# A two-layer graph transformer on one core: the second table laid out by rank, stored by ScalarE's queue, and the edges' node numbers turned into ranks on TensorE

## The chip, the cores and the metric

The kernel runs on one core of a Trainium2 chip. The metric is the device time of one execution in microseconds (us), the median of three runs. One execution was also recorded by the hardware profiler, and every statement about where time goes rests on that record. The engines are called as in the profile: PE is TensorE (PEld its weight loads), DVE is VectorE, ACT is ScalarE, POOL is GpSimd, and SP is SyncE, which here only issues DMAs.

## The reference, cut to what matters

There are 6250 nodes of 128 features and 100,000 edges. A node has one of 16 types, an edge one of 32. Two layers run one after the other; in each, with 8 heads of 16 features:

```
k, q, v = x @ Wk[type], x @ Wq[type], x @ Wv[type]          # per node
kT = einsum('nhd,htdo->nhto', k, Watt)                      # per node and edge type
vT = einsum('nhd,htdo->nhto', v, Wmsg)
a  = (kT[src, :, etype] * q[dst]).sum(-1) * pri[:, etype].T / 4
att = softmax of a over the edges that end in the same node
hag = segment_sum(vT[src, :, etype] * att, dst)
h  = silu(hag @ Wa[type])
h  = h * sigmoid(skip[type]) + x * (1 - sigmoid(skip[type]))
x  = layernorm(h) * g + b
```

The output is `layernorm(x0 + (x2 @ ff_w + ff_b))`, where x0 is the input and x2 the result of the second layer.

## The kernel before

**Tables.** For each layer l the kernel writes a table `tabs[l]` in HBM. A node has 32 rows in it, one for each edge type, and a row holds the 128 numbers of kT and the 128 of vT (1 KB). One table has 6272 x 32 rows, 205 MB. An edge is served by gathering row `32 * node(src) + etype`. These row numbers are made once, in `kvi`, and are put into the tile `ell` (128 partitions, one column per slot) during the preparation.

**Ranks, blocks and superblocks.** The nodes are sorted into ranks 0 to 6271 by class of type and number of incoming edges (`rank_order`, lines 641 to 863). A block is 128 consecutive ranks, one per partition; there are 49 blocks, and block b has `KB[b]` slots, which is how many incoming edges its nodes may have (block 44, called `TOP`, has 28 slots of gathers and a way of its own for the rest). Over all blocks there are 819 slots. One slot is one indirect DMA of POOL that fetches 128 rows, one per partition (line 1324). Blocks are grouped into 15 superblocks of two to four (`sbs`, lines 1073 to 1087), with 83, 63, 37, 48, 83, 63, 37, 39, 83, 63, 37, 37, 63, 37 and 46 slots, in this order of work.

**Preparation (0 to 652 us).** It sorts the nodes, builds the first table (PE products in `table_block`, copies from PSUM to the tile `st`, scatters by POOL at line 1024), and fills `ell`, `neg` and the like (`limits_of`, lines 865 to 947, runs in steps beside the gathers of `ell`).

**Edges (`edges`, line 1127), once per layer.** For each block the slots are gathered in groups of four into one of twelve buffers `kv` (line 1320). After each gather POOL sets two small tiles `pause` to zero (line 1330). VectorE multiplies a group by the query (line 1344) and sums per head (line 1350). When a block's scores are complete, `finished` (line 1189) runs in steps beside the next block: maximum, exponential on ScalarE (line 1213), weighted sums of the vT half (lines 1229 to 1257). So a group's buffer is held until the next block is under way. In layer 1 the query, the exponentials and the products sit in a PSUM tile of two banks, a pair, from the pool `tps`, which has three such pairs (`query`, line 1171).

**Nodes (`nodes`, line 1426).** When a superblock's last block is done, its node work is put on the list `work` and goes on in steps beside the next superblock: normalization, typed product with Wa, tanh, layer norm. In layer 0 it also makes the next k, v and q and hands k and v to `pieces_of` (line 1568), which makes the second table's rows for that superblock; in layer 1 it ends with the last product and the result.

**The second table's way to HBM.** `pieces_of` walks through `table_block` (line 262): for each block twice (16 edge types at a time) PE makes the products in pairs of `tps`, ScalarE copies them to `st` (line 281; 2 MB, three buffers), and the tile is put on a list `late`. Eight steps later `scatter` (line 1555) lets POOL write it with an indirect DMA to the rows of the nodes, whose numbers are in `row2`. All 98 scatters must have landed before the first gather of layer 1.

**What sets the order.** POOL's instructions run in the order written in the code. On the other engines a scheduler orders them at compile time, following the order of the code; at run time each engine works strictly in order and waits on semaphores. `tick` (line 1140) decides in which slot a step of `work` or `pieces` is written: each entry has a pace in steps per slot, and only the first entry of a list moves.

The steps of the prediction touch lines 1324 and 1330 (gather and pause), 1344 and 1350 (products and sums per slot group), 1213 (exponential), 274 and 281 (table products and copies), 1556 (scatter), 1177 (query into a pair), 237 and 251 (typed products), 1519 and 1123 (rows h and q out and back in by SP), 1525 and 1527 (last bias and residual).

## Time and profile before

| | us |
|---|---|
| median of three runs | 3402.58 (3395.8 to 3412.61) |
| profiled execution | 3402.78 |
| its span, first to last instruction | 3400.7 |
| preparation | 0 to 652 |
| gathers of layer 0 | 652 to 2050 |
| tail of layer 0 | 2050 to 2120 |
| gathers of layer 1 | 2120 to 3351 |
| tail of layer 1 | 3351 to 3401 |

The stages are read from the first and last gather of each layer. A row of a group in the profile gives line, engine, operation, output and inputs, shape and count, then after a bar the busy time in us and the mean of one in ns, then after a second bar the engine's idle time just before these instructions and what ended most of it. "issue" as a releaser means that the record shows nothing that the engine waited for, and "remote" a semaphore whose source it does not show. A row of the waits gives who waited for whom, the total in us, how often, and the longest.

### The profile page before, as it was taken

How to read it: one execution, taken by the hardware profiler on the slowest of the kernel's cores; microseconds unless marked ns; L12 is line 12 of the kernel's file. 1: busy time of each engine (PE TensorE's matmuls, PEld its weight loads, DVE VectorE, ACT ScalarE, POOL GpSimd, SP SyncE). 2: the span in 40 equal slices, each digit the busy share in tenths (PEclk: the TensorE clock that was granted, in tenths of full speed). 3: DMA queues.
4: the chain of work that ended last, by engine and by line, in shares of the span. 5: the costliest groups of instructions: out<-in, count | busy, mean ns of one | idle time of the engine just before them, and what ended most of it. 6: DMA issues, size and time to landing. Idle time of an engine off the chain costs nothing. (4 is left out here: it accounts for less than half of the span.)

```text
span 3400.7 us, 24784 instructions
## 1 busy us (share of the span) xinstructions
PE 1668.8 (49%) x5291; PEld 745.2 (22%) x5291; DVE 1864.6 (55%) x4307; ACT 1035.4 (30%) x1720; POOL 2394.8 (70%) x5400
## 2 busy tenths in 40 slices
PE   5899999403676657776667565011211122012112
PEld 2444444201232322232222222000110011001001
DVE  8626642156655666566655543356555565566555
ACT  2778754200444123423334434001100120012111
POOL 2232367588878877788777772888788888888874
PEclk8888976556676768777777667555555555555555
DMA  6899989833677456766667768333333333333331
GB/s 178 364 417 412 406 324 347 272 89 95 236 260 269 140 183 250 270 243 211 215 246 277 269 241 320 99 94 99 99 95 97 98 107 100 90 101 100 92 88 45
DMA packets 169096, 674.80 MB, mean 198 GB/s; under 512 B 52972, under 2 KB 83726, under 8 KB 143886
## 3 DMA queue, kind: packets, MB, share of 16 engines
q0 software_dynamic: 114144, 638.40, 52.7%
q1 hardware_dynamic: 38402, 27.55, 2.9%
q10 hardware_dynamic: 16384, 7.11, 0.9%
q14 instruction: 120, 0.98, 0.1%
q8 instruction: 46, 0.75, 0.1%
HBM read 248.64 MB, written 425.02 MB: 198 GB/s over the span
## 5 line engine op out<-in xcount | busy, mean ns | idle before, releaser
L1324 POOL DMA_INDIRECT kv<-tab,ell x1638 | 1639.9, 1001 | 339.3 <-issue 286.0
L281 ACT COPY st<-tb 128x512 f32<-128x512 f32 (+1 forms) x1108 | 745.1, 761 | 548.2 <-PE tb L274 275.2
L1344 DVE TENSOR_TENSOR kv<-kv,tb 128x512 f32<-128x512 f32 (+3 forms) x223 | 142.9, 641 | 466.6 <-DMA kv<-tab,ell 446.5
L1330 POOL MEMSET pause<- 128x32 bf16 x3276 | 335.0, 141 | 67.9 <-remote 49.7
L259 PE MATMUL nb<-ident,hag 128*128 128x128 f32 x98 | 25.5, 396 | 714.7 <-DVE hag L1391 576.5
L1024 POOL DMA_INDIRECT tab<-st,rows x98 | 100.1, 1021 | 280.0 <-ACT st L281 251.2
L274 PE MATMUL tb<-bdv,kvT 32*128 32x512 f32 x784 | 254.0, 815 | 86.4 <-ACT st L281 53.7
L1350 DVE TENSOR_REDUCE a<-kv 128x32 f32<-128x512 f32 (+2 forms) x446 | 281.7, 634 | 6.9 <-DVE den L1219 1.2
L274 PE MATMUL tb<-bdv,vT 32*128 32x512 f32 x784 | 270.1, 782 | 8.6 <-ACT st L281 6.5
L251 PE MATMUL nb<-xm,wa 128*128 128x512 f32 (+2 forms) x336 | 191.7, 730 | 159.0 <-DVE xm L237 113.7
L274 PE MATMUL tb<-bdk,kvT 32*128 32x512 f32 x784 | 246.8, 809 | 42.7 <-ACT st L281 24.0
L1344 DVE TENSOR_TENSOR kv<-kv,q 128x512 f32<-128x512 f32 (+3 forms) x223 | 142.6, 642 | 215.5 <-DMA kv<-tab,ell 199.2
L274 PE MATMUL tb<-bdk,kT 32*128 32x512 f32 x784 | 242.6, 806 | 6.7 <-ACT st L281 3.0
L237 DVE SCALAR_TENSOR_TENSOR xm<-ntb,nb 128x512 f32<-128x512 bf16 (+2 forms) x304 | 156.4, 562 | 141.9 <-remote 85.8
L1556 POOL DMA_INDIRECT tab<-st,row x98 | 107.8, 1100 | 172.0 <-ACT st L281 139.4
L259 PEld LDWEIGHTS nb<-ident,hag 128*128 128x128 f32 x98 | 15.2, 196 | 733.9 <-issue 538.5
L1503 PE MATMUL nb<-xm,wkqv 128*128 128x512 f32 (+2 forms) x312 | 150.2, 646 | 45.0 <-DVE xm L237 30.9
L1177 ACT COPY tb<-hq 128x128 f32<-128x128 f32 x49 | 13.1, 269 | 460.0 <-DVE sums L1257 325.0
L251 PEld LDWEIGHTS nb<-xm,wa 128*128 128x128 f32 x336 | 88.4, 281 | 262.3 <-DVE xm L237 133.8
L251 PE MATMUL nb<-xm,wq 128*128 128x384 f32 (+2 forms) x168 | 84.5, 653 | 119.0 <-DVE a L1201 91.4
L259 PE MATMUL nb<-ident,hs 128*128 128x128 f32 x98 | 35.3, 464 | 218.0 <-DVE hs L1464 157.0
L274 PEld LDWEIGHTS tb<-bdv,vT 32*128 32x128 f32 x784 | 109.7, 221 | 107.6 <-ACT st L281 68.8
(336 smaller groups left out, 2740.3 us busy)
## 6 DMA issues: line engine op xcount, KB each, us to landing
kv<-tab,ell POOLq DMA_INDIRECT x1638
hr<-xrd SPq DMA_DIRECT2D x14, 256.0 KB
hqd<-hs SPq DMA_DIRECT2D x7, 512.0 KB
hq<-hqd SPq DMA_DIRECT2D x7, 512.0 KB
xrd<-xr POOLq DMA_DIRECT2D x10, 256.0 KB
hr<-xrd SPq DMA_DIRECT2D x10, 192.0 KB
hqd<-hs SPq DMA_DIRECT2D x5, 384.0 KB
hq<-hqd SPq DMA_DIRECT2D x5, 384.0 KB
```

The lines of the kernel that those rows point to most:

```text
L237: nc.vector.scalar_tensor_tensor(xm[:, :n], ntb[:, :n], float(t), hT[:, :n], op0=ALU.is_equal, op1=ALU.mult)
L251: nc.tensor.matmul(ps[:, :n], w[:, t, :], xm[:, :n], start=(t == types[0]), stop=(t == types[-1]))
L259: nc.tensor.transpose(tr[:, i * P:(i + 1) * P], src_of(i), ident)
L274: nc.tensor.matmul(pt[:, b], yT[s, i * P:(i + 1) * P], bd[s, tt, :], start=True, stop=True)
L281: nc.scalar.copy(to, pt)
L1024: put = nc.gpsimd.indirect_dma_start(out=tabs[0].rearrange("(n t) c -> n (t c)", t=16), out_offset=bass.IndirectOffsetOnAxis(ap=rows1[:, t ...
L1324: get = nc.gpsimd.indirect_dma_start(out=kv[:, j - j0, :], out_offset=None, in_=tabs[l][:], in_offset=bass.IndirectOffsetOnAxis(ap=ell[:, ...
L1330: nc.gpsimd.memset(pause[:, at % PAUSES, half], 0.0)
L1344: nc.vector.tensor_tensor(kk, kk, of.unsqueeze(1).to_broadcast([P, c, D]), op=ALU.mult)
L1350: nc.vector.tensor_reduce(to, kk.rearrange("p k (h d) -> p k h d", h=H), axis=AX.X, op=ALU.add)
L1503: nc.tensor.matmul(ps[:, :n], wkqv[:, j, t, :], xm[:, :n], start=(t == types[0]), stop=(t == types[-1]))
L1556: put = nc.gpsimd.indirect_dma_start(out=tabs[1].rearrange("(n t) c -> n (t c)", t=16), out_offset=bass.IndirectOffsetOnAxis(ap=row2[:, tg ...
```

## The change

The second table is laid out by rank and no longer by node. A superblock's ranks are consecutive, so a stored tile of 128 nodes goes to 128 places with a fixed distance of 32 KB, and a plain DMA on ScalarE's queue, issued right after the tile's last copy, takes the place of POOL's indirect DMA eight steps later. The list `late`, the function `later` and the tile `row2` go.

The numbers in `ell` name nodes, which serves layer 0. For layer 1 they are turned into ranks, in place, by a new generator `found`, one call per superblock. It splits each number into edge type (5 bits), node within 128 (low) and node's hundred-and-twenty-eight (high, 0 to 48). For a group of up to four slots, PE spreads the low parts over 128 partitions (four matmuls with the identity), and subtracts the 49 possible high parts from the high part (two matmuls); ScalarE takes the sign of row number against low part, and the square of 96 times the difference; PE adds the square and the products of the signs with `steps_of` (one matmul and two for each slot), where `steps_of` holds half the differences of the rank table from row to row, so that the signs add up to the wanted entry; VectorE takes the minimum over the 49 columns, in which all but the right one are pushed up by the square, and writes the rank to `ell`. At the end the number becomes 32 * rank + etype.

`found` has four steps per group and is written on a third list `finds` of `tick`. While layer 0 works on its second and third superblock, the first and second are converted; while layer 1 works on superblock s, superblock s + 2 is.

PSUM: `tps` becomes three pairs by name, handed out in turn. In layer 0 all three are in the turn, for `found` too; in layer 1 two are, and the third is kept for `found`.

Smaller parts: the rank table's differences are made in `limits_of` (`turn`, `steps_of`); the layer-norm weights `gt` and `bt` hold one layer only and are loaded anew at the start of layer 1, on SP; the last bias is loaded to all partitions and added with the identity as the other operand in place of a row of ones.

```diff
+    steps_of = keep.tile([P, 2, NT], BF16, name="steps_of")
...
+    def load_norm(l):
+        nc.sync.dma_start(gt, ln_g[l:l + 1, :].to_broadcast([P, D]))
+        nc.sync.dma_start(bt, ln_b[l:l + 1, :].to_broadcast([P, D]))
...
+            turn = pp2.tile([P, 3, P], F32, name="turn", tag="rv", bufs=1)
+            nc.vector.tensor_scalar(turn[:, 0], colf, rowf, 1.0, op0=ALU.subtract,
+                                    op1=ALU.is_equal)
+            nc.vector.tensor_scalar(turn[:, 1], colf, rowf, -float(P - 1), op0=ALU.subtract,
+                                    op1=ALU.is_equal)
+            nc.vector.tensor_tensor(turn[:, 2], ident, turn[:, 0], op=ALU.subtract)
+            nc.vector.tensor_tensor(turn[:, 2], turn[:, 2], turn[:, 1], op=ALU.add)
+            turn_ps = pps.tile([P, 2, NT], F32, name="ps")
+            nc.tensor.matmul(turn_ps, turn[:, 2], partf, start=True, stop=True)
+            yield
+            for i in range(2):
+                nc.vector.tensor_scalar(steps_of[:, i], turn_ps[:, i], (0.5, P / 2)[i], None,
+                                        op0=ALU.mult)
...
-        tps = ctx2.enter_context(tc.tile_pool(name="tps", bufs=3, space=PSUM))
+        tps = ctx2.enter_context(tc.tile_pool(name="tps", bufs=1 if fast else 3, space=PSUM))
+
+        class Turns:
+            def __init__(self):
+                self.of, self.at = 3, 0
+            def tile(self, shape, dtype, name):
+                self.at = (self.at + 1) % self.of
+                return tps.tile(shape, dtype, name=f"tb{self.at}")
+
+        pairs = Turns() if fast else tps
...
+            if l:
+                pairs.of = 2
...
             def tick(n):
-                if late and not pieces:
-                    idle[0] += 4 / PIECE * n
-                    while idle[0] >= 1.0:
-                        idle[0] -= 1.0
-                        later()
-                for of in (work, pieces):
+                for of in (work, pieces, finds):
...
+                ahead = s + 2 if l else s - 1
+                if 0 <= ahead < (len(sbs) if l else 2):
+                    n = slots(ahead)
+                    finds.append([found(l, *sbs[ahead][:2]), (4 * -(-n // CH) + 2) / (0.9 * slots(s)),
+                                  0.0])
...
-            nc.tensor.matmul(f[:, :n].rearrange("p (i d) -> p i d", i=k), one_row,
-                             ffb.unsqueeze(1).to_broadcast([1, k, D]), start=True, stop=False)
+            nc.tensor.matmul(f[:, :n].rearrange("p (i d) -> p i d", i=k), ident,
+                             ffb.unsqueeze(1).to_broadcast([P, k, D]), start=True, stop=False)
...
+        def stored(tg, st, b):
+            put = nc.scalar.dma_start(
+                tabs[1].rearrange("(n g t) c -> g n (t c)", g=TG, t=16)[tg, b * P:(b + 1) * P, :],
+                st.rearrange("p t c -> p (t c)"))
+            for other in puts:
+                tc.declare_no_dep(put.ins, other.ins, reason="rows of other nodes")
+            puts.append(put)
...
             for i in range(k):
                 def store(tg, st, b=i0 + i):
-                    late.append([8, (tg, st, b)])
-
-                yield from steps(table_block(ep, tps, kT, vT, i, share, STB, store,
-                                             2 if fast else 1))
-            while late and not fast:
-                later()
+                    (stored if fast else scatter)(tg, st, b)
+
+                for _ in table_block(ep, pairs, kT, vT, i, share, STB, store, 2 if fast else 1):
+                    yield
+                    yield
+
+        def found(l, i0, k):
+            n = sum(GB[i0:i0 + k])
+            assert n <= FIND and CH * NT <= 2 * P
+            at = slice(KO[i0], KO[i0] + n)
+            whole = npl.tile([P, CH * P // 2], I32, name="side")[:, :3 * n].rearrange(
+                "p (a k) -> p a k", a=3)
+            nc.vector.tensor_scalar(whole[:, 0], ell[:, at], 5, P - 1, op0=ALU.arith_shift_right,
+                                    op1=ALU.bitwise_and)
+            nc.vector.tensor_single_scalar(whole[:, 1], ell[:, at], 12, op=ALU.arith_shift_right)
+            nc.vector.tensor_single_scalar(whole[:, 2], ell[:, at], RT - 1, op=ALU.bitwise_and)
+            part = npl.tile([P, 3, FIND], BF16, name="parts")[:, :, :n]
+            nc.vector.tensor_copy(part, whole)
+            yield
+            for j0 in range(0, n, CH):
+                c = min(CH, n - j0)
+                ps = (tps.tile([P, 2, SB * P], F32, name="tb2") if l else
+                      pairs.tile([P, 2, SB * P], F32, name="tb"))
+                for j in range(c):
+                    nc.tensor.matmul(ps[:, 0, j * P:(j + 1) * P],
+                                     part[:, 0, j0 + j:j0 + j + 1].to_broadcast([P, P]), ident_b,
+                                     start=True, stop=True)
+                off = ps[:, 1, :c * NT]
+                nc.tensor.matmul(off, ident_b,
+                                 part[:, 1, j0:j0 + c].unsqueeze(2).to_broadcast([P, c, NT]),
+                                 start=True, stop=False)
+                nc.tensor.matmul(off, ident_b,
+                                 minus_col.unsqueeze(1).to_broadcast([P, c, NT]),
+                                 start=False, stop=True)
+                yield
+                side = npl.tile([P, CH, P], BF16, name="side")
+                nc.scalar.activation(side[:, :c].rearrange("p k e -> p (k e)"), ps[:, 0, :c * P],
+                                     AF.Sign, bias=half_row)
+                far = npl.tile([P, CH * NT], BF16, name="far")
+                nc.scalar.activation(far[:, :c * NT], off, AF.Square, scale=96.0)
+                yield
+                ranks = ps[:, 1, 2 * P:2 * P + c * NT]
+                nc.tensor.matmul(ranks, ident_b, far[:, :c * NT], start=True, stop=False)
+                for j in range(c):
+                    for i in range(2):
+                        nc.tensor.matmul(ps[:, 1, 2 * P + j * NT:2 * P + (j + 1) * NT],
+                                         side[:, j], steps_of[:, i], start=False,
+                                         stop=(i + j == c))
+                yield
+                nc.vector.tensor_reduce(ell[:, at][:, j0:j0 + c],
+                                        ranks.rearrange("p (k i) -> p k i", k=c),
+                                        axis=AX.X, op=ALU.min)
+                yield
+            nc.vector.scalar_tensor_tensor(ell[:, at], ell[:, at], float(RT), part[:, 2],
+                                           op0=ALU.mult, op1=ALU.add)
+            yield
...
             else:
                 load_typed(wa, Wa[1])
+                load_norm(1)
```

More of the change, by code (lines that the diff above doesn't have):

```diff
@@ L209, in load_later @@
         nc.sync.dma_start(wa, Wa[0].rearrange("t d o -> d t o"))
[L210 to L212 removed]
+        load_norm(0)
         nc.sync.dma_start(ffw, ff_w)
[L214 to L215 removed]
+        nc.sync.dma_start(ffb, ff_b.unsqueeze(0).to_broadcast([P, D]))
     def superblocks(n):
@@ L1183, in moved @@
                 n = what.shape[1]
-                ps = pair[:, 1, D:D + n] if pair is not None else tps.tile(
+                ps = pair[:, 1, D:D + n] if pair is not None else pairs.tile(
                     [P, 2, SB * P], F32, name="tb")[:, 0, :n]
@@ L1372, in edges @@
                 put_out(*results.pop(0)[1])
-            while work or pieces or late:
-                if late and not pieces:
-                    later()
-                for of in (work, pieces, pieces, pieces):
+            while work or pieces or finds:
+                for of in (work, finds, pieces, pieces, pieces):
                     if of and next(of[0][0], of) is of:
@@ L1544, in nodes @@
                     put_out(o, i0, i)
-        late = []
-        def later():
-            for what in late:
-                what[0] -= 1
-            while late and late[0][0] <= 0:
-                scatter(*late.pop(0)[1])
         def scatter(tg, st, b):
-            put = nc.gpsimd.indirect_dma_start(
+            at = npl.tile([P, 1], I32, name="scatter_at", bufs=2)
+            nc.vector.tensor_scalar(at, node[:, b:b + 1], float(TG), float(tg),
+                                    op0=ALU.mult, op1=ALU.add)
```

50 lines of the change are left out of this document (20 added, 30 removed).

## The prediction

> **What bounds the kernel now.** I read the page first, then the busy time by stage, then for each stage what POOL, VectorE and ScalarE waited for.
>
> ```profile
> span 3400.7 us, 24784 instructions
> PE 1668.8 (49%) x5291; PEld 745.2 (22%) x5291; DVE 1864.6 (55%) x4307; ACT 1035.4 (30%) x1720; POOL 2394.8 (70%) x5400
> ```
>
> The whole says little: POOL is the busiest, at 70%. The stages say more (columns: busy us of PE, weight load, DVE, ACT, POOL with counts, then granted clock, DMA share, GB/s).
>
> ```profile
> 652.00:2050.00 1398.00, 855.12 (x2554) 351.54 (x2554) 798.50 (x1702) 467.87 (x622) 1114.80 (x2543) 0.70 0.62 218
> 2050.00:2120.00 70.00, 40.69 (x156) 19.07 (x156) 26.51 (x54) 30.03 (x42) 10.15 (x13) 0.71 0.86 343
> 2120.00:3351.00 1231.00, 206.00 (x449) 104.78 (x449) 690.33 (x1674) 137.93 (x277) 998.46 (x2500) 0.54 0.34 97
> ```
>
> The first row is layer 0's 819 gathers, the second its tail, the third layer 1's 819 gathers. Equal gathers, but layer 0 takes 1398 us and layer 1 1231. POOL's groups from 652 to 2110, with the ends of the stage:
>
> ```profile
> L1324 POOL DMA_INDIRECT kv<-tab,ell x819 | 852.6, 1041 | 162.8 <-issue 131.9 <-SPq L1753 14.8 <-DVE kv L1344 2.7
> L1330 POOL MEMSET pause<- 128x32 bf16 x1638 | 167.3, 141 | 11.1 <-remote 7.8 <-issue 2.6
> L1556 POOL DMA_INDIRECT tab<-st,row x98 | 107.8, 1100 | 172.0 <-ACT st L281 139.4 <-issue 16.5 <-ACT q L1108 7.8
> L1324 POOL DMA_INDIRECT kv<-tab,ell x1638: 950/952/4532, 651.8 to 3350.3; - x182
> 2050.16 0.20 POOL L1330 MEMSET pause<- 128x32 bf16 x2
> ```
>
> The last column is POOL's idle time ahead of the group. The scatters of the second table (L1556) cost 107.8 us of work and 172.0 of waiting, nearly all of it for ScalarE's copies into st. Gathers are hardly ever held by VectorE (2.7 us). So layer 0 is bound by POOL, standing in front of scatters. In layer 1 POOL has no scatters, and VectorE waits for gathers:
>
> ```profile
> DVE kv L1344 <- DMA kv<-tab,ell: 199.2, 73, 8.4
> DVE xm L237 <- remote: 95.8, 17, 18.5
> DVE den L1219 <- ACT a L1213: 92.4, 18, 22.6
> DVE kv L1344 <- issue: 15.9, 7, 4.7
> DVE kv L1344 <- DMA kv<-tab,ell: 446.5, 142, 21.0
> DVE kv L1344 <- issue: 19.9, 16, 2.8
> ACT st L281 <- issue: 114.4, 26, 19.3
> ACT st L281 <- remote: 83.4, 30, 6.5
> ACT st L281 <- DMA tab<-st,row: 9.8, 5, 3.1
> ```
>
> The first four and the last three rows are of layer 0, the middle two of layer 1. ScalarE's copies lose up to 207.6 us ahead of st, much of it, as I read it, because st is freed only when a scatter lands, and the scatter stands behind gathers in POOL's order. It is a ring: POOL waits for the copy, the copy for an older scatter.
>
> **The change part by part.** The sum is made against the profiled execution: 3402.8 us, span 3400.7 with 2.1 around it, 0.2 above the median of the three runs.
>
> *Scatters leave POOL.* POOL's floor in layer 0 is gathers 852.6 + pauses 167.3 + idle before gathers 162.8 less the 14.8 ahead of the first + 11.1 = 1179.0. The stage ran from 651.8 to 2050.4, 1398.6, so at most 219.6 goes. What is late next is VectorE: 1398.6 less its waits for gathers, 199.2 + 15.9, is 1183.5 with every other wait kept.
>
> *Rank look-up in layer 0.* Superblocks 0 and 1 (83 and 63 slots, 21 + 16 groups of four) are converted here, the other thirteen (174 groups) in layer 1. Prices:
>
> ```profile
> L1438 ACT ACTIVATE th<-nb 128x512 f32<-128x512 f32 x7 | 4.2, 597 | 46.5 <-PE nb L251 38.8 <-issue 7.7
> L1213 ACT ACTIVATE tb<-a 128x200 f32<-128x200 f32 x4 | 1.4, 341 | 76.5 <-DVE m L1206 38.9 <-DVE a L1208 36.6 <-issue 1.0
> L1219 DVE TENSOR_REDUCE den<-tb 128x8 f32<-128x200 f32 x4 | 1.4, 357 | 0.0
> 29.42 1.55 PE L408 MATMUL ps<-col,row 128*128 128x98 bf16 x17 [13.18 <-DVE col L403]
> 27.00:40.00 13.00, 4.65 (x50) 1.00 0.87 193
> 2098.92 1.19 PE L274 MATMUL tb<-bdk,kvT 32*128 32x512 f32 x8 [0.18 <-DVE st L279]
> L188 ACTq DMA_DIRECT2D bdk<-in_L_gnn_Watt_dram x16: 318/433/5252, 4.8 to 674.4; - x16
> ```
>
> A group's minimum (128x4 from 196 columns of PSUM) is nearest to den's 0.357 us; with five small operations per superblock at about 0.26 (the same row, shorter) that is 37 x 0.357 + 2 x 1.3 = 16 us of VectorE in layer 0, whose floor becomes 1199.5, and 174 x 0.357 + 13 x 1.3 = 79 in layer 1.
>
> *How near to the floors.* VectorE is fed through twelve kv buffers, and a group's buffer is held until the next block is under way, so POOL can lead by four or five groups only. Both floors, 1179 and 1199.5, lie close, and the waits of the one will not all fall inside those of the other. Layer 1, bound by POOL, still shows POOL waiting for others:
>
> ```profile
> POOL pause L1330 <- remote: 41.9, 21, 3.0
> POOL kv L1324 <- DVE acc L1229: 8.6, 1, 8.6
> POOL kv L1324 <- DVE kv L1344: 1.8, 2, 1.5
> ```
>
> That is 52.3 us; I add half, 26, between nothing and all of it. Layer 0's stage becomes 1225.5: **-173**. From below, xm's 95.8 and den's 92.4 could shrink with the ring gone, but POOL's 1179.0 then holds: -219.6. From above, only the work of the scatters goes (below).
>
> *Stores on ScalarE's queue.* 98 issues; ACT's earlier DMA issues take 0.32 to 5.25, median 0.43: 42 us on an engine busy 468 of 1398. Behind each stand copies and exponentials (L1213), at most 49 x 0.43 = 21 us for den if one stood ahead of every exponential. I take 0, since the 207.6 us of ScalarE's waits shrink; the cover gone, it costs 21. The store waits only for ScalarE's own copies, which precede it, and st is free sooner. Bytes stay.
>
> *Look-up in layer 1.* Per group PE gets 15 pairs of load and matmul: seven of 128 or 196 columns, eight of 49. 17 pairs of 98 columns took 1.55 us at clock 1.00, 0.091 each. Seven at 0.091 x 1.6 plus eight at about 0.075 is 1.6, and 2.7 at a clock of 0.6 (bounds: 15 x 0.091 = 1.4; all 196 wide at 0.54, 5.1). ScalarE adds Sign (0.597) and Square (0.341), no table load more in its order. With three handoffs of 0.18 a group's chain is 2.7 + 0.94 + 0.36 + 0.54 = 4.5 us. Totals: PE 470 beside 206 busy of 1231, ACT 163 beside 138. VectorE's minimum waits for the chain, and behind it in order stand the kv products that free buffers; but VectorE has 466.4 us of waits for gathers to give, against 79. The next group's first matmul waits for that minimum (one PSUM pair is kept for it), and layer 1's node matmuls queue behind: a microsecond or two, paid from the same 466. A gather now also waits for its superblock's ranks. By the order of the changed kernel on VectorE these are done 5 to 27 groups of gathers before they are read; at 1231/224 = 5.5 us per group the tightest places (5 and 6 groups) leave 27 us. Where sixteen look-ups stand beside eleven groups of gathers, 16 x 4.5 = 72 us meet 60, a lag of 12, within the lead. I take **+10**, between 0 and 3 stretches x 12 = 36.
>
> *The rest, at 0.* Two buffers instead of three for the query pair: ScalarE's copy already waits for the sums of the block before, and two blocks are alive. Bias by identity: the two rows below cost the same. Six VectorE operations more in the preparation lie ahead of a wait of 23.71 us for the first table's last scatter; without it, 2 us. Two loads of 64 KB at layer 1's start stand on SP ahead of the hq loads, which wait for st in any case. The tail: ten scatters, then 12.4 us until the last has landed; a store must land as well.
>
> ```profile
> L1525 PE MATMUL nb<-ffb,one_row 1*128 1x512 f32 (+2 forms) x30 | 26.4, 980 | 0.0
> L1527 PE MATMUL nb<-hr,ident 128*128 128x512 f32 (+2 forms) x30 | 26.1, 974 | 0.0
> 650.71 0.06 DVE L1067 MEMSET eps<- 128x1 f32 x1 [23.71 <-DMA tab<-st,rows]
> 2107.17 0.97 POOL L1556 DMA_INDIRECT tab<-st,row  x1 [5.41 <-issue]
> 2120.54 1.00 POOL L1324 DMA_INDIRECT kv<-tab,ell  x1 [12.40 <-issue]
> ```
>
> Sum: 3402.8 - 173 + 10 = **3240**.
>
> **The rivals.** *A, only the issue is saved.* The waits for st move from POOL to VectorE and ScalarE, because the copies and not the queue set the pace. Then the stage loses 88 of the 98 scatters' work (ten lie in the tail), 88 x 1.1 = 97: 3402.8 - 97 + 10 = 3316. For it: PE is busy 61% at clock 0.70 and gets 37 x 2.7 = 100 us more. Against it: ScalarE itself waits for scatters to land. The Trainium skill, "DMA: Bandwidth & Descriptors", section "Issuing engines are not separate DMA queues", says the same thing as a rule: another issuing engine saves only the sequencer's time. By that rule, the time would be A's.
>
> *B, POOL's floor is reached.* VectorE's waits behind ScalarE go too: 3402.8 - 219.6 + 10 = 3193.
>
> *C, the look-up holds VectorE in layer 1.* For each of 174 groups VectorE stands still for most of the chain. It has 466.4 - 79 = 387 us to give, 2.2 us a group; above that layer 1 grows by 174 us per us, and from (387 + 173)/174 = 3.2 us of the 4.5 on, the kernel is slower than before. At 4: 174 x 4 - 387 = 309, and 3402.8 - 173 + 309 = 3539. For it: the minima stand two to five VectorE operations apart. Against it: three yields lie between a chain's start and its end.
>
> *D, the direct stores land slowly.* 2.1 MB at the tail's 343 GB/s is 6.1 us. If rank order, with rows 32 KB apart one after the other, took double, 12.2, then 98 x 12.2 + 107 MB of gathers at 343 GB/s (313) = 1509 us, +111 on the stage: 3402.8 + 111 + 10 = 3524, slower from 11.0 us a store on. No row here shows a direct store of this size. The Trainium skill, same page, section "Latency and other measured facts", reports copies that fall from 207 to 103 GB/s as the row pitch grows from 512 KiB to 4 MiB; 32 KiB is below its range.
>
> *E, no effect:* the ring closes elsewhere (ScalarE's store, then st) at the old pace: 3402.8, with the 10 of layer 1 3413.
>
> **How the numbers follow.** Forecast 0.55 (its own range 3200 to 3290), A 0.17, B 0.13, C 0.08, D 0.03, E 0.04. The range reaches from under B to over A, 3175 to 3335, and holds 0.85; C, D and E lie outside. Within 0.5% is 3386 to 3420, about what a measurement of this kernel can tell from no change. Faster 0.55 + 0.17 + 0.13 = 0.85, same 0.04, slower 0.11.
>
> **What would show it.** Layer 0's gathers should take 1180 to 1260 us, with POOL's idle before gathers near 160 and VectorE's wait for gathers far under 199. ScalarE's wait ahead of st should fall under 100. In layer 1 the stage should stay within 1231 to 1270, VectorE's wait for gathers falling from 446 to 250 to 350; under 100, with long waits for PE at the minimum, is C. A store's landing above 11 us is D. It is wrong if POOL waits long for VectorE in layer 0 (kv buffers), or if gathers wait for ranks.

## The result, and the profile after

The changed kernel takes **3792.34 us** (median of four runs, 3780.32 to 3807.55); the kernel before took 3405.77 us (3395.80 to 3412.61) beside it. The ratio is 1.114, 95% interval 1.1088 to 1.1192: slower, where 3240 us had been forecast with a range of 3175 to 3335. The profiled execution is the one of 3780.32 us. Its page begins:

```profile
span 3778.4 us, 31798 instructions
PE 1902.5 (50%) x8383; PEld 956.6 (25%) x8383; DVE 1915.6 (51%) x4599; ACT 1216.0 (32%) x2142; POOL 2307.8 (61%) x5302
```

All engines but POOL have more work, and POOL, 87 us lighter, is busy for a smaller share. By stage (columns as in the prediction; the stages are again cut at the first and last gather of each layer):

```profile
645.00:2179.00 1534.00, 836.30 (x2891) 365.40 (x2891) 790.31 (x1728) 461.83 (x647) 1039.47 (x2455) 0.67 0.54 189
2179.00:2304.00 125.00, 103.12 (x409) 45.28 (x410) 35.41 (x83) 70.86 (x95) 0.62 (x3) 0.77 0.80 317
2304.00:3730.00 1426.00, 402.47 (x2954) 275.58 (x2951) 740.74 (x1907) 284.26 (x621) 997.46 (x2502) 0.56 0.29 84
```

Layer 0's gathers take 1534 us where they took 1398, its tail 125 where it took 70, layer 1's gathers 1426 where they took 1231. These are +136, +55 and +195; with a preparation shorter by 7 and an end shorter by 1 that is the difference of the spans, 378 us. All three stages got worse, so there is more than one thing to find.

The waits of layer 0 in the changed kernel, from 645 to 2179 us:

```profile
POOL kv L1361 <- DVE acc L1261: 314.6, 14, 102.8
DVE kv L1381 <- DMA kv<-tab,ell: 260.8, 78, 8.1
ACT st L288 <- PE tb L281: 188.4, 86, 25.4
ACT st L288 <- issue: 118.4, 19, 22.7
ACT st L288 <- remote: 97.8, 20, 17.2
DVE xm L244 <- PE nb L266: 81.1, 16, 26.2
```

Lines are those of each kernel's own file; in the changed one 1361 is the gather, 1381 a group's first product, 1261 and 1268 the later ones, 288 the copy into st, 1644 and 1657 Sign and minimum of a look-up. POOL no longer waits for ScalarE's copies. It waits 314.6 us for buffers that VectorE holds, where 2.7 us was the largest such share in the row of before. And VectorE, fed by a freer POOL, waits longer for gathers than before, 260.8 against 199.2. Both cannot come from one engine being too slow on average: sometimes POOL runs ahead of VectorE and stands, and later VectorE finds nothing fetched. ScalarE still stands ahead of st, for PE now.

Three groups of layer 1, the gathers, the first product of a group and the minimum of a look-up (from 2310 to 3730 us):

```profile
L1361 POOL DMA_INDIRECT kv<-tab,ell x815 | 782.0, 960 | 333.4 <-issue 138.4 <-DVE tb L1261 61.9 <-DVE tb L1268 28.0
L1381 DVE TENSOR_TENSOR kv<-kv,tb 128x512 f32<-128x512 f32 (+3 forms) x221 | 140.2, 638 | 113.4 <-DMA kv<-tab,ell 87.5 <-issue 15.0 <-ACT side L1644 8.1
L1657 DVE TENSOR_REDUCE ell<-tb 128x4 int32<-128x196 f32 (+2 forms) x172 | 60.7, 353 | 428.7 <-remote 351.9 <-PE tb L1653 67.3 <-issue 4.7
```

VectorE's wait for gathers fell from 446.5 us to 87.5, and 428.7 us of waiting stand ahead of the minimum: the sign that the prediction had named for rival C.

The longest wait of POOL can be followed in the timeline. Its columns are start, duration, engine, line, operation, output and inputs, count, and the idle time before. These are rows of VectorE, with POOL's next gather at the end:

```profile
1006.38 0.69 DVE L1381 TENSOR_TENSOR kv<-kv,q 128x512 f32<-128x512 f32 x1 [2.98 <-DMA kv<-tab,ell]
...
1010.38 1.88 DVE L244 SCALAR_TENSOR_TENSOR xm<-ntb,nb 128x512 f32<-128x512 bf16 x3 [0.81 <-PE nb L266]
...
1019.68 0.36 DVE L1657 TENSOR_REDUCE ell<-tb 128x4 int32<-128x196 f32 x1 [5.67 <-PE tb L1653]
1029.09 0.36 DVE L1657 TENSOR_REDUCE ell<-tb 128x4 int32<-128x196 f32 x1 [9.04 <-PE tb L1653]
...
1066.02 1.95 DVE L244 SCALAR_TENSOR_TENSOR xm<-ntb,nb 128x384 f32<-128x384 bf16 x4 [13.71 <-PE nb L266]
1080.30 0.55 DVE L1480 SCALAR_TENSOR_TENSOR th<-th,nb 128x384 f32<-128x384 f32 x1 [12.33 <-ACT th L1473]
...
1106.61 0.69 DVE L1261 TENSOR_TENSOR acc<-kv,a 128x512 f32<-128x512 f32 x1
1107.57 1.16 POOL L1361 DMA_INDIRECT kv<-tab,ell  x1 [102.80 <-DVE acc L1261]
...
2295.89 0.33 ACTq L1593 DMA_DIRECT2D tab<-st  x1
2304.15 0.95 POOL L1361 DMA_INDIRECT kv<-tab,ell  x1 [124.52 <-DMA tab<-st]
```

For a hundred us VectorE takes no ordinary group of gathers. Its queue holds one step of node work after another and eight minima, each waiting for PE or ScalarE, and the products of the groups that lie ready stand behind them in order. That is a matter of the order in the queue. Counted in the traces of layer 0, the most VectorE instructions between the first product of one group and that of the next are 32 in the kernel before and **67** in the changed kernel; gaps with 30 and more are 1 and 12. (The expectations below name 23 and 66, and 19 and 17 for the order as written; they count the compiled program by another rule. By the count of the traces the written order has 24 to 26.) Look-ups stand beside only two of layer 0's fifteen superblocks, and the changed kernel without any (e1, below) has the same 67, so these are not what fills the gaps. The last two rows of the fence bear on rival D: the last store is issued at 2295.89, and the first gather of layer 1, which waits for all stores, starts 8.26 us later.

### The profile page after: what moved, and what is told of

Read it like the earlier page. It is cut to its first block, busy times and chain, and to the rows that moved or that the text cites. A ratio compares the mean times of both kernels' runs of the same rounds, so it can differ in the third digit from the quotient of the medians.

```text
span 3778.4 us, 31798 instructions
## 1 busy us (share of the span) xinstructions
PE 1902.5 (50%) x8383; PEld 956.6 (25%) x8383; DVE 1915.6 (51%) x4599; ACT 1216.0 (32%) x2142; POOL 2307.8 (61%) x5302
## 3 DMA queue, kind: packets, MB, share of 16 engines
q14 instruction: 126, 1.03, 0.1%
## 5 line engine op out<-in xcount | busy, mean ns | idle before, releaser
L1361 POOL DMA_INDIRECT kv<-tab,ell x1638 | 1661.4, 1014 | 955.0 <-DVE acc L1261 336.0
L1644 ACT ACTIVATE side<-tb,half_row 128x512 bf16<-128x512 f32 (+2 forms) x211 | 142.2, 674 | 870.9 <-remote 459.2
L1632 PE MATMUL tb<-ident_b,parts 128*128 128x128 bf16 x819 | 112.0, 280 | 540.0 <-DVE ell L1657 225.2
L1657 DVE TENSOR_REDUCE ell<-tb 128x4 int32<-128x196 f32 (+2 forms) x211 | 74.5, 353 | 537.6 <-remote 405.2
L281 PE MATMUL tb<-bdv,kvT 32*128 32x512 f32 x784 | 280.5, 809 | 87.9 <-ACT st L288 68.0
L1381 DVE TENSOR_TENSOR kv<-kv,q 128x512 f32<-128x512 f32 (+3 forms) x223 | 141.0, 642 | 314.4 <-DMA kv<-tab,ell 260.8
L1650 PE MATMUL tb<-far,ident_b 128*128 128x196 bf16 (+2 forms) x211 | 64.1, 304 | 453.5 <-ACT far L1647 221.9
L281 PE MATMUL tb<-bdv,vT 32*128 32x512 f32 x784 | 279.4, 780 | 10.9 <-ACT st L288 8.9
L281 PE MATMUL tb<-bdk,kvT 32*128 32x512 f32 x784 | 256.6, 797 | 17.6 <-ACT st L288 8.1
L1632 PEld LDWEIGHTS <-parts 128*128 128x128 bf16 x819 | 81.8, 124 | 581.1 <-issue 468.5
L1653 PEld LDWEIGHTS <-side 128*128 128x128 bf16 x1638 | 96.4, 116 | 482.9 <-issue 480.5
L1381 DVE TENSOR_TENSOR kv<-kv,tb 128x512 f32<-128x512 f32 (+3 forms) x223 | 141.1, 636 | 113.4 <-DMA kv<-tab,ell 87.5
```

The costliest lines, as they stand in the source:

```text
L281: nc.tensor.matmul(pt[:, b], yT[s, i * P:(i + 1) * P], bd[s, tt, :], start=True, stop=True)
L1361: get = nc.gpsimd.indirect_dma_start(out=kv[:, j - j0, :], out_offset=None, in_=tabs[l][:], in_offset=bass.IndirectOffsetOnAxis(ap=ell[:, ...
L1381: nc.vector.tensor_tensor(kk, kk, of.unsqueeze(1).to_broadcast([P, c, D]), op=ALU.mult)
L1632: nc.tensor.matmul(ps[:, 0, j * P:(j + 1) * P], part[:, 0, j0 + j:j0 + j + 1].to_broadcast([P, P]), ident_b, start=True, stop=True)
L1644: nc.scalar.activation(side[:, :c].rearrange("p k e -> p (k e)"), ps[:, 0, :c * P], AF.Sign, bias=half_row)
```

## The experiments

Theory L: the look-up's chain holds VectorE, and the gathers with it. Rival S: the direct stores make layer 0 slower by themselves. A third, theory O, came up with the first results: the stores cost nothing, but without the scatters the scheduler orders VectorE's queue in blocks.

The later runs were on other chips than the first pair. On these the kernel before takes 3197 to 3201 us, so each run is compared with the kernel before on its own chip. The stages are us between the first and the last gather of a layer.

| run | ratio (95% interval) | gathers, layer 0 | tail | gathers, layer 1 |
|---|---|---|---|---|
| first pair: kernel before | 1 | 1398 | 70 | 1231 |
| first pair: changed kernel | 1.114 (1.1088 to 1.1192) | 1534 | 125 | 1426 |
| e1 no look-ups | 1.0483 (1.0461 to 1.0506) | 1393 | 124 | 1148 |
| e2 look-ups alone | 1.0035 (1.0018 to 1.0053) | 1309 | 71 | 1144 |
| e3 no minimum | 1.0563 (1.0533 to 1.0593) | 1412 | 127 | 1148 |
| e4 look-ups in layer 1 only | 1.0457 (1.0436 to 1.0479) | 1391 | 123 | 1143 |
| e5 changed kernel again | 1.0521 (1.0503 to 1.0539) | 1426 | 127 | 1144 |
| e6 changed, VectorE as written | 0.9871 (0.9855 to 0.9888) | 1241 | 77 | 1173 |
| e7 no look-ups, VectorE as written | 0.9679 (0.9650 to 0.9709) | 1203 | 79 | 1137 |
| e8 before, VectorE as written | 0.9915 (0.9899 to 0.9932) | 1276 | 72 | 1138 |
| e9 stand-in for the scatters | 1.0433 (1.0406 to 1.0460) | 1422 | 78 | 1150 |
| e10 changed, as written in layer 0 | 0.9835 (0.9798 to 0.9872) | 1230 | 81 | 1144 |
| e11 changed, no pauses | 1.0246 (1.0226 to 1.0266) | 1365 | 126 | 1096 |
| e12 = e10 without pauses | 0.9533 (0.9509 to 0.9557) | 1200 | 82 | 1096 |

**e1: the stores without the look-ups.**

```diff
-                ahead = s + 2 if l else s - 1
+                ahead = -1
...
-            if l:
-                pairs.of = 2
```

> This kernel keeps the direct stores of the changed kernel and leaves all look-ups out (layer 1 then gathers rows by node numbers out of a table by rank, so its values are not the reference's), with three PSUM pairs in layer 1 as before. Theory L (the look-up's chain TensorE-ScalarE-TensorE-VectorE holds VectorE, and the gathers through it): the loss is gone, the stores give what the forecast gave them or some of it, 3200 to 3320 us. Rival S (the stores on ScalarE's queue make layer 0 slower by themselves, as 1.81 us per gather from 1110 to 2180 us against 1.71 before suggests): 3400 to 3550 us.

Measured 3351.43 us. Its stages:

```profile
636.00:2029.00 1393.00, 735.27 (x2343) 316.15 (x2344) 777.44 (x1678) 424.91 (x573) 1046.36 (x2457) 0.69 0.59 208
2029.00:2153.00 124.00, 92.61 (x368) 38.96 (x367) 33.87 (x80) 68.27 (x90) 0.42 (x1) 0.82 0.80 320
2153.00:3301.00 1148.00, 181.41 (x449) 99.75 (x449) 687.29 (x1674) 138.25 (x277) 997.25 (x2500) 0.55 0.36 104
```

The loss in layer 0 and in its tail is there without one look-up, and so are POOL's long waits for VectorE, from 636 to 2029 us:

```profile
POOL kv L1359 <- DVE acc L1259: 205.6, 15, 76.0
```

Theory L falls for layer 0, and S is left for the time being.

**e2: the look-ups without the stores.** The list `late` and GpSimd's scatters are put back, the rest stays as changed. The row numbers of a scatter are made just before it, since `row2` no longer has room.

```diff
-                    (stored if fast else scatter)(tg, st, b)
+                    at = npl.tile([P, 1], I32, name="scatter_at", bufs=3)
+                    nc.vector.tensor_scalar(at, node[:, b:b + 1], float(TG), float(tg),
+                                            op0=ALU.mult, op1=ALU.add)
+                    late.append([8, (at, st)])
```

> This kernel has the look-ups of the changed kernel, but the pieces go out by GpSimd's indirect scatters as before (the table is then by node number and is read by rank, so its values are not the reference's). Theory L: layer 1 stays as slow as in the changed kernel (1426 us of gathers) and layer 0 loses about 100 us to its two look-ups: 3700 to 3900 us. Rival S: 3400 to 3500 us.

Measured 3206.64 us:

```profile
635.00:1944.00 1309.00, 870.34 (x3103) 380.82 (x3103) 819.57 (x1843) 497.07 (x695) 1116.83 (x2545) 0.72 0.67 233
1944.00:2015.00 71.00, 44.25 (x188) 21.23 (x187) 27.56 (x63) 31.74 (x45) 10.03 (x12) 0.72 0.87 341
2015.00:3159.00 1144.00, 404.30 (x2965) 279.71 (x2962) 744.49 (x1908) 286.16 (x623) 997.82 (x2502) 0.57 0.36 105
```

All 211 look-ups together cost 0.35%, and layer 1 with 174 of them takes 1144 us, no more than the 1148 of e1 without any. Theory L is wrong on this chip altogether. That left a question: why had layer 1 lost 195 us in the first pair?

**e3: the look-ups without VectorE's minimum.**

```diff
-                nc.vector.tensor_reduce(ell[:, at][:, j0:j0 + c],
-                                        ranks.rearrange("p (k i) -> p k i", k=c),
-                                        axis=AX.X, op=ALU.min)
                 yield
-            nc.vector.scalar_tensor_tensor(ell[:, at], ell[:, at], float(RT), part[:, 2],
-                                           op0=ALU.mult, op1=ALU.add)
```

> The changed kernel without VectorE's part behind the ranks: the minimum of each group and the last operation of each superblock are left out, so the node numbers stay in place; TensorE's and ScalarE's part of each look-up stays. If what costs is that VectorE waits in line for the ranks (537.6 us ahead of the minimum in all, theory L), layer 1 goes back to about 1250 us and layer 0 loses less: 3400 to 3560 us. If the look-up costs through TensorE, ScalarE or the PSUM pair that it takes from the others, the time stays within 2% of 3792 us.

Measured 3377.68 us, about as slow as e5. On this chip the wait for the ranks is not what costs.

**e4: no look-ups in layer 0.**

```diff
-                if 0 <= ahead < (len(sbs) if l else 2):
+                if l and ahead < len(sbs):
```

> The changed kernel without the two look-ups in layer 0 (37 of 211 groups; two superblocks are then gathered by node numbers, and the values are not the reference's). From 820 to 1110 us, with those two look-ups, a gather took 2.69 us for 108 gathers, against 1.71 on average before. Theory L: about 100 us are gone from there and some from the tail of layer 0: 3640 to 3710 us. Rival S: under 40 us, 3750 us and more.

Measured 3342.35 us, a ratio of 1.0457 against 1.0521 with them (e5, on another chip): the two look-ups of layer 0 cost some 0.6%, or 20 us, by the ratios and 35 us by the stage (1391 against 1426), and not 100.

The absolute numbers in the expectations of e1 to e4 were set for the first chip, where the kernel before takes 3406 us. Taken as ratios to that, only e2 falls into one of its ranges (S, 1.00 to 1.03). e1 with 1.048 lies above both of its ranges (0.94 to 0.98 and 1.00 to 1.04), e3 with 1.056 between its two (1.00 to 1.05, and 1.09 and more), and e4 with 1.046 under both (1.07 to 1.09, and 1.10 and more).

**e5: the changed kernel on another chip.** No edit.

> The changed kernel unchanged, on the chip of these runs, since the runs so far lay on a chip where the kernel before took 3197 us and not 3405. There the stores alone gave 1.048, the stores with the look-ups of layer 1 1.046, and the look-ups alone 1.004. If the parts add up: 1.05 to 1.07 of the kernel before. If the part that came on top on the first chip (1.114) belongs to the kernel and not to the chip: 1.10 to 1.12.

Measured 3372.26 us; the parts add up, and what came on top of them in 1.114 was not seen again on another chip. The stages, and layer 1's product and minimum as above:

```profile
635.00:2061.00 1426.00, 812.98 (x2892) 361.81 (x2893) 790.25 (x1728) 458.42 (x647) 1051.90 (x2456) 0.68 0.58 204
2061.00:2188.00 127.00, 105.14 (x413) 45.68 (x414) 34.95 (x82) 70.79 (x95) 0.46 (x3) 0.76 0.79 312
2188.00:3332.00 1144.00, 399.58 (x2945) 276.19 (x2944) 744.70 (x1908) 285.17 (x621) 997.77 (x2502) 0.58 0.36 105
```

```profile
L1381 DVE TENSOR_TENSOR kv<-kv,tb 128x512 f32<-128x512 f32 (+3 forms) x221 | 141.6, 642 | 319.6 <-DMA kv<-tab,ell 311.8 <-ACT tb L1209 3.4 <-issue 2.9
L1657 DVE TENSOR_REDUCE ell<-tb 128x4 int32<-128x196 f32 (+2 forms) x172 | 60.4, 351 | 42.0 <-PE tb L1653 39.3 <-ACT h L1558 2.0
```

The same program waits 42.0 us ahead of the minimum here and 428.7 on the first chip. What differs can be read from the first chip's timeline, where PE's matmuls end and their readers do not start:

```profile
2846.19 0.54 PE L1653 MATMUL tb<-steps_of,side 128*128 128x49 bf16 x8
...
2848.42 0.68 DVE L1261 TENSOR_TENSOR tb<-kv,tb 128x512 f32<-128x512 f32 x1
2854.38 0.36 DVE L1657 TENSOR_REDUCE ell<-tb 128x4 int32<-128x196 f32 x1 [5.28 <-remote]
...
2855.34 0.37 PE L1639 MATMUL tb<-minus_col,ident_b 128*128 128x196 bf16 x1
...
2861.49 0.69 ACT L1644 ACTIVATE side<-tb,half_row 128x512 bf16<-128x512 f32 x1 [15.46 <-remote]
```

The ranks are done at 2846.73, VectorE is free from 2849.10, and the minimum starts at 2854.38; the next group's differences are done at 2855.71 and ScalarE's Sign starts at 2861.49. A reader starts when a semaphore, a counter that PE raises at the end of a matmul, has come far enough. The trace also holds the times of these signals. PE runs no matmul from 2846.73 to 2854.80, and yet signals of it come in that time, one by one, at 2847.26, 2849.35, 2852.88 and 2854.29; the minimum starts after the last of these, and Sign after one at 2861.41. So it is the signals that are late, and "remote" in the rows stands for them, since the profile finds no instruction that ended near them.

I counted PE's signals from the first gather on, and called one late if it is recorded over 1 us after the end of PE's latest signalling matmul. On the first chip 538 of 2734 are late in the changed kernel and 195 of 1213 in the kernel before; of VectorE's signals 4 of 2634 and 26 of 2269 are late by the same rule, of ScalarE's 2 of 972 and 2 of 566. In each of the twelve traces of e1 to e12, on four other chips, 2 of PE's are late, both at the very end of the program. On the first chip late signals are more frequent where POOL had been working for 8 us and more without a break of 1 us (357 of 839 in the changed kernel, against 181 of 1895 elsewhere). But in e5 the same program has 2629 signals in such stretches, and none is late. (The counts in the expectation of e11 are of readers and not of signals; they point the same way.) Lateness of PE's signals is not all that sets the first chip apart: the kernel before has only 13 late signals of 141 in layer 1, and still takes 1231 us there against 1138 in e8 (with VectorE's order as written).

**e6, e7, e8: VectorE's order as written.** This is the test of theory O. `manual_schedule` takes an engine out of the scheduler's hands; the kernel had it for GpSimd only.

```diff
-            ctx2.enter_context(tc.manual_schedule(engines={mybir.EngineType.Pool}))
+            ctx2.enter_context(tc.manual_schedule(engines={mybir.EngineType.Pool, mybir.EngineType.DVE}))
```

It is put on the changed kernel (e6), on e1 (e7) and on the kernel before (e8).

> The changed kernel with VectorE's instructions in the order in which the kernel writes them, as GpSimd's already are, in place of the scheduler's order. In layer 0 up to 66 other VectorE instructions stand between two gather multiplies in the changed kernel, 23 at most in the kernel before, 19 in this one. Theory O (the stores cost nothing by themselves; without the scatters the scheduler puts a superblock's node work in blocks, and VectorE stands in them while gathers wait): layer 0's gathers fall to 1200 to 1300 us, 0.94 to 1.00 of the kernel before. Rival S (the stores are slow by themselves: they land late or slow the gathers): within 2% of the changed kernel, 1.04 and more.

> The kernel with direct stores and no look-ups (layer 1 gathers by node numbers out of a table by rank, so its values are not the reference's), with VectorE's order as written. Theory O: 0.93 to 0.98 of the kernel before, where the scheduler's order gave 1.048. Rival S: 1.03 to 1.06.

> The control: the kernel before with VectorE's order as written. Theory O: its order was spread already (23 other instructions at most between two gather multiplies, 17 here), so within 2% of the kernel before. If the written order is faster or slower by itself, the same difference shows here and is taken off the two runs beside it.

Measured 3164.43, 3097.99 and 3174.45 us. Layer 0 of the three, in this order, each from its own kernel:

```profile
637.00:1878.00 1241.00, 824.94 (x3045) 364.94 (x3046) 796.49 (x1744) 485.94 (x682) 1037.72 (x2457) 0.75 0.68 243
```

```profile
637.00:1840.00 1203.00, 749.28 (x2508) 321.77 (x2512) 785.59 (x1698) 455.23 (x610) 1039.45 (x2455) 0.75 0.70 251
```

```profile
638.00:1914.00 1276.00, 823.80 (x2554) 343.52 (x2554) 791.01 (x1701) 464.42 (x621) 1110.54 (x2545) 0.72 0.68 239
```

The same stores that lost 4.8% in the scheduler's order (e1) gain 3.2% in the written one (e7), and still 2.4% (0.9679/0.9915) against the kernel before in the same order (e8), with layer 0 shorter by 73 us. The written order alone gives the kernel before 0.85%. On these chips rival S falls and theory O stands: nothing but VectorE's order was edited between e1 and e7, or between e5 and e6. The scheduler then also places PE's and ScalarE's instructions anew around it, so what is shown is the effect of VectorE's order with what follows from it. POOL's waits for VectorE show it in one pair of rows, layer 0 of e5 and of e6:

```profile
POOL kv L1361 <- DVE acc L1261: 234.4, 15, 102.7
```

```profile
POOL kv L1361 <- DVE acc L1261: 53.8, 5, 25.5
```

In layer 1 the written order is worse by 29 us where there are look-ups (1173 in e6 against 1144 in e5).

**e9: a stand-in for the scatters.** The direct stores stay; at each place of a scatter GpSimd copies a strip of st. This brings back the scheduler's even order without taking VectorE from it.

```diff
+        def stand(tg, st, b):
+            rest = npl.tile([P, 32], F32, name="rest", bufs=2)
+            nc.gpsimd.tensor_copy(rest, st[:, 0, :32])
...
                     (stored if fast else scatter)(tg, st, b)
+                    if fast:
+                        late.append([8, (tg, st, b)])
```

> Direct stores from ScalarE's queue, no look-ups (layer 1 gathers by node numbers out of a table by rank, so its values are not the reference's), the scheduler's order for VectorE; but at each place where the kernel before has a scatter, GpSimd copies a 128x32 strip of the finished piece into a tile that nobody reads. With that the scheduler again puts 23 other VectorE instructions at most between two gather multiplies of layer 0 (66 without it). Theory O: 0.96 to 1.00 of the kernel before, where the same kernel without the strip copies gave 1.048. Rival S (the stores are slow by themselves) or a gain that only the written order gives: 1.03 to 1.06.

Measured 3333.80 us, a ratio of 1.0433: not theory O's range but the one named for its rivals. The tail is back at 78 us, but layer 0 takes 1422. Its waits:

```profile
DVE kv L1384 <- DMA kv<-tab,ell: 486.9, 128, 13.9
...
POOL rest L1607 <- ACT st L288: 206.2, 40, 17.9
```

The strip copy waits for ScalarE's copies into st, 206.2 us in all, and holds the gathers behind it, so VectorE waits 486.9 us for them. The stand-in has put a wait on POOL that hides what it was to show, so this run decides nothing between O and its rivals. It shows at least that a small number of instructions between gather products (24 at most in its trace) does not by itself make the stage short.

**e10: the written order where it helps.** The changed kernel, with VectorE's order as written in layer 0 only.

```diff
-            if fast:
+            if fast and l == 0:
+                with tc.manual_schedule(engines={mybir.EngineType.Pool, mybir.EngineType.DVE}):
+                    edges(l)
+            elif fast:
                 edges(l)
```

> The changed kernel, complete, with VectorE's order as written in layer 0 alone and the scheduler's order in layer 1. With the written order in both layers, layer 0's gathers took 1241 us and layer 1's 1173; with the scheduler's order layer 1's took 1144. Theory O: the two add up, 3130 to 3150 us or 0.98 of the kernel before, a little below 0.987. If the order of one layer carries over into the other: 0.985 and more.

Measured 3145.77 us, as expected. The interval of the ratio, 0.9798 to 0.9872, does not exclude 0.985, but the stages speak for independent layers: layer 1 takes 1144 us as in e5, and layer 0 near e6's 1241:

```profile
635.00:1865.00 1230.00, 817.57 (x3051) 362.58 (x3052) 797.13 (x1748) 487.18 (x683) 1034.59 (x2455) 0.75 0.69 246
```

**e11: do frequent gathers make PE's results late?**

```diff
-                            for half in range(2):
-                                nc.gpsimd.memset(pause[:, at % PAUSES, half], 0.0)
```

> The changed kernel without the two memsets of GpSimd behind each gather, so that gathers can follow each other in about 1.1 us in place of 1.4; the order on VectorE is the same. On the first chip TensorE's results reached their readers over 1.9 us late in 131 of 282 cases where GpSimd had issued gathers for 8 us and more, and in 18 of 337 otherwise; on the chips of the experiments in 8 of 411. Theory P (the rate of gathers makes the results late, and the first chip is only nearer to the point where it starts): the share of late results goes up to 20% and more, and layer 1's gathers take longer than 1144 us in spite of the shorter issue. Rival (it is a matter of the chip alone): the share stays under 5%, and layer 1's gathers take 1000 to 1100 us.

Measured 3274.21 us, with layer 1's gathers at 1096. Of PE's 3220 signals 2 are late, those at the end, so theory P falls for these chips: the rate alone does not do it. The pauses cost time here.

**e12: both together.**

> The changed kernel, complete, with VectorE's order as written in layer 0 (0.9835 with that alone) and without the two memsets behind each gather (which took 0.027 off the ratio of the changed kernel: 1.052 to 1.025). If the two are independent: layer 1's gathers 1096 us in place of 1145 and layer 0's a little under 1230, 0.96 to 0.97 of the kernel before. Rival: with the written order GpSimd is close to VectorE's pace already, and faster gathers only wait for buffers: 0.98 and more, with GpSimd's waits for VectorE in layer 0 well above the 77 us of the run with pauses.

Measured **3054.67 us**, 0.9533 of the kernel before, faster than both kernels and a little better than expected:

```profile
634.00:1834.00 1200.00, 821.60 (x3031) 364.53 (x3032) 795.12 (x1743) 483.77 (x679) 844.05 (x819) 0.75 0.71 251
1834.00:1916.00 82.00, 57.12 (x277) 26.22 (x278) 34.51 (x68) 45.56 (x63) 0.23 (x1) 0.83 0.89 355
1916.00:3012.00 1096.00, 395.76 (x2945) 273.02 (x2944) 743.77 (x1907) 284.42 (x620) 827.12 (x864) 0.58 0.38 109
```

POOL's gathers now wait longer for VectorE's later products than in e10 (75.7 us against 45.3 in layer 0), as the rival said, but both layers are still shorter. How much the kernel before would gain by the same two edits was not measured.

## Why the prediction was wrong, point by point

*Scatters leave POOL, and how near to the floors (-173).* This is the step that failed. It took VectorE's queue as it was and subtracted the waits that would go. But the queue is written anew by the scheduler when the scatters leave, and in the new order POOL waits 314.6 us for VectorE: layer 0 became 136 us longer. That such an order makes the stage long is shown on the other chips, where 1393 us (e1) became 1203 (e7) with nothing but VectorE's order edited, on two chips where the kernel before differs by 0.1%. On the first chip the order was not held in any run. There the same program also gets PE's signals late, and how the 136 us divide between the two stays open.

The size of the step failed too. With the order held in both kernels the stage gained 73 us (e8 against e7), where the step had 173. That layer 0 of the changed kernel then takes 1230 us (e10, forecast 1225.5), and 1200 without the pauses (e12, the VectorE floor had been put at 1199.5), is luck: those chips start from 1276 us (e8) and not from 1398, and e12 has one edit more. What the step needed was a second look at the compiled order on VectorE, where gaps of this length could be seen before any run.

*What the stores save.* Of the 172.0 us that POOL stood ahead of scatters, 124.0 lie in the stage itself. On another chip, with VectorE's order as written (e8), the 88 scatters of the stage stand for 23.9:

```profile
L1556 POOL DMA_INDIRECT tab<-st,row x88 | 97.7, 1110 | 23.9 <-issue 11.8 <-ACT st L281 11.5 <-ACT a L1213 0.5
```

So most of the wait that the step took off was not seen again there. In e7 the 97.7 and 23.9 us are gone, but the gathers work longer (875.1 us against 848.6) and idle longer ahead of them (173.6 against 152.3): 74 us remain, the 73 of the stage. POOL's work there falls by 71 us (1110.54 to 1039.45). That is rival A's reasoning, that only the issue is saved, with a smaller size than its 97. The Trainium skill, "DMA: Bandwidth & Descriptors", section "Issuing engines are not separate DMA queues", gives it as a rule, and these runs agree.

*Stores on ScalarE's queue at 0.* The issue is cheap, 0.36 us on average. But ScalarE's waits ahead of st did not fall under 100 us: 188.4 behind PE, 118.4 "issue" and 97.8 "remote" were read. The ring of scatters was only a part of what the prediction read as one. In e8, with scatters, the copies wait for them 69.0 us:

```profile
ACT st L281 <- DMA tab<-st,row: 69.0, 21, 8.9
```

There is no "remote" ahead of st there, so the 83.4 us before were most likely late signals of PE. With the stores the wait for scatters is gone, and the wait for PE is longer (217.1 in e7 against 113.0 in e8).

*Look-up in layer 1 (+10).* On the other chips, with the scheduler's order, it was right within its bounds: 1144 us with look-ups (e2, e5) and 1148 without (e1), with VectorE's wait for gathers at 311.8 in e5 (250 to 350 expected). In the written order the look-ups cost 36 us there (1173 in e6 against 1137 in e7). On the first chip the sign of rival C came true, and the stage grew by 195 us, though not by the price of the chain's instructions: 428.7 us of waiting ahead of 172 minima is 2.5 us each, above the 2.2 that C had named as free, because PE's signals were late. C's own sum would give only some 45 us for that; it gave away all of VectorE's waits for gathers, of which 113.4 us stayed. That late signals lie behind the difference is read from two traces of one program. It was not made to come and go by an edit, and why the first chip's signals are late stays open.

*Look-up in layer 0.* The step had 16 us of VectorE's work. Between e4 and e5 the stage grows by 35 us, and between e7 and e6, on one chip with the order held, by 38: about twice that.

*The tail at 70.* It became 125, and 124 in e1. As I read it, VectorE's blocks leave more pieces undone when the last gather is issued; in the written order the tail is 77 to 82 with the stores.

*The rivals.* D falls: besides the 8.26 us after the last store, the page of e7 gives 7.9 us as the median from a store's issue to its landing, under D's 11.0 (the row ends with it):

```profile
tab<-st ACTq DMA_DIRECT2D x98, 2048.0 KB, 7.9
```

B and E were not seen. The case that happened in layer 0, the same work in a worse order, was on no list; "it is wrong if POOL waits long for VectorE in layer 0" was the only hint at it.

## What to carry to other kernels

Where a scheduler orders the other engines, taking instructions off one queue changes the order on all of them: look at the compiled order of the bottleneck's neighbours, and count what stands between two steps of the critical loop, before pricing the change by the old order's waits. Then test the change with the order held, in both kernels. A chain that crosses engines several times per step should be priced with a spare for late handoffs, since the same minimum waited 2.5 us each time on one chip and 0.2 on another.

## What the runs showed of the hardware

- On the first chip many of PE's signals to the other engines are recorded over 1 us after PE's latest signalling matmul: 538 of 2734 in the changed kernel, 195 of 1213 in the kernel before, and two in each trace of the other chips. Of VectorE's and ScalarE's in the changed kernel hardly any are (4 of 2634 and 2 of 972). The cause is open.
- One program differs by 6% between chips: the kernel before takes 3406 us on the first and 3197 to 3201 on the others.
- A direct store of 2 MB, 128 rows of 16 KB at a distance of 32 KB, landed 7.9 us after its issue in the median (e7).
